# Layer 3: biases folded into the weights' last row, and a second bank for the attention sums

## The chip, the cores and the metric

The kernel runs on one core of one Trainium2 chip. The metric is the device time of one execution in microseconds; the median of three runs stands for a kernel. A core has five engines with instruction queues of their own: PE (matrix multiply, with its weight loads shown apart as PEld), DVE (vector), ACT (scalar functions), POOL (GpSimd) and SP (which issues most DMAs here). PE writes its results to PSUM, which the kernel uses as eight banks of 512 fp32 values per partition.

## The reference, cut to what matters

The model has four layers over x of shape (4, 56, 56, 128): 4 images of 3136 tokens with 128 channels. Layers 0 to 2 (neighbourhood attention; a selective scan; additive attention and a layer of 64 experts that choose their tokens) are not changed. Layer 3 is:

```python
t = t + _L3_attn_ref(_ln_t(t))     # softmax(x x^T) x, per image
t = t + _L3_ffn_ref(_ln_t(t), router_w, router_b, expert_w, expert_b)

def _L3_ffn_ref(x, router_w, router_b, expert_w, expert_b):     # 8 experts, the best 2 of a token
    router_probs = softmax(x @ router_w + router_b, axis=-1)
    top_p, top_i = top_k(router_probs, 2)
    top_p = top_p / sum(top_p, axis=-1, keepdims=True)
    expert_out = einsum('bnd,edc->bnec', x, expert_w) + expert_b
    gathered = take_along_axis(expert_out, top_i[..., None], axis=2)
    return einsum('bnk,bnkc->bnc', top_p, gathered)
```

`_ln_t` subtracts the mean over the channels and divides by the deviation, without a gain or an offset. So the 128 channels of a normalised token add up to zero, and its last channel is minus the sum of the other 127.

## The kernel before

All tokens stay in SBUF as X[b], one tile of [112, 28, 128] fp32 for each image: 28 tiles of 112 tokens. A chunk is four such tiles, 448 tokens; an image has seven (NCH = 7).

The attention of layer 3 (from L1462) works on units (b, c, t): for chunk c of queries and key tile t of 128 keys (25 of them, the last with 64), "weights" (L1545) multiplies the transposed tokens to scores in a "q" bank, and ACT takes their exp into a tile "e"; "weighted" (L1555) multiplies the keys by e into the sums "o" of the chunk, over 25 units into one bank. The pool of "o" has one bank (L1485), that of "q" two, "m" (shared by transposes and small products) two, "pe" (experts) two, and "h" one. The last serves only the pass over layer 2's experts for the last image, which is woven into the first part of layer 3. That makes eight.

The order on PE, ACT, DVE and POOL is written out by hand. A list `at` holds steps by slot; the loop (L1593) runs in each turn u the scores of unit u, the sums of unit u - 2, and then the steps of slot u - 2. A chunk's steps start in the slot of its last unit:

- slot 0, "copied" (L1530): the sums leave their bank, the first half by DVE (L1533), the second by ACT (L1534). Slots 2 and 3, "added" (L1536): transposed back by matmuls with "back" (L1149), divided, added to X.
- slots 4 to 12, "normed_chunk" (L1609): statistics, root, Newton step, norm of the tokens (slot 8), transposes (slot 11), copy by ACT to f_xT.
- slots 14 to 17: the router's matmuls with addition of its bias and the maximum ("route", L1663), exp, and the choice of two experts, which makes the gate, an [112, 4, 8] tile with zeros for the experts not chosen ("choose", L1687).
- slot 22, "turn_gate" (L1703): four transposes of the gate on PE; slot 23: ACT copies them to gT; slot 25, "biases" (L1714): four matmuls of gT with the experts' biases, and one DVE addition to X.
- slots 25, 27, 29 and 31, "experts" (L1722): for each of the four tiles, two matmuls against four experts at a time, and eight gated additions to X on DVE (L1731). Slot 33: the chunk is stored.

A chunk has 25 slots, so slots 25 and up fall together with the next chunk's slots 0 and up, and stand ahead of them in the same slot. Each fp32 matmul appears in the trace as two instructions.

The next image's chunks are prepared (normed_chunk, then "keys", L1510) during the present image. The pass over layer 2's experts is fed in by a counter u, at half a slot or more per step (L1587), and ends in slot 291 of some 730.

The weights of layer 3 are loaded by SP in L1472 to L1480. Before the loop stands a start (L1565 to L1567), in which the first image's seven chunks are normed and turned, one after the other.

Of the kernel before, what the change touches and what calls it, by code (L numbers as in the profile page):

```python
# [11 lines left out]
ALU = mybir.AluOpType  # L12
AX = mybir.AxisListType
PSUM = bass.MemoryType.PSUM
# [3 lines left out]
B, HW, C = 4, 56, 128  # L18
S = HW * HW
P = 128  # L20
TP = 2 * HW
NT = S // TP
TC = 4
CH = TC * TP
# [28 lines left out]
E3, K3 = 8, 2  # L53
# [51 lines left out]
class Hybrid:  # L105
# [1356 lines left out]
    def layer3(self):  # L1462
# [6 lines left out]
        with ExitStack() as ctx:  # L1469
            wp = ctx.enter_context(tc.tile_pool(name="l3_w", bufs=1))  # L1470
            w = {}
            w["rw"] = self.load(wp, [P, E3], "rw", a["L3_ffn_router_w"])  # L1472
            w["rb"] = self.load(wp, [TP, E3], "rb", a["L3_ffn_router_b"].partition_broadcast(TP))
            w["ew"] = self.load(wp, [P, E3, C], "ew", a["L3_ffn_expert_w"].rearrange("e d c -> d e c"))
            w["eb"] = self.load(wp, [E3, C], "eb", a["L3_ffn_expert_b"])
            shift = self.t(wp, [P, 1], "shift")
            nc.vector.memset(shift, SHIFT3)
            w["eps"] = self.t(wp, [TP, 1], "eps3")
# [5 lines left out]
            ps_q = ctx.enter_context(tc.tile_pool(name="l3_q", bufs=2, space=PSUM))  # L1484
            ps_o = ctx.enter_context(tc.tile_pool(name="l3_o", bufs=1, space=PSUM))  # L1485
            ps_m = ctx.enter_context(tc.tile_pool(name="l3_m", bufs=2, space=PSUM))
            ps_h = ctx.enter_context(tc.tile_pool(name="l3_h", bufs=1, space=PSUM))
            ps_e = ctx.enter_context(tc.tile_pool(name="l3_e", bufs=2, space=PSUM))
            ctx.enter_context(
                tc.manual_schedule(engines={ET.PE, ET.Activation, ET.DVE, ET.Pool})  # L1490
            )
# [62 lines left out]

            def weighted(b, c, t):  # L1555
                if t == 0:
                    po[b, c] = self.t(ps_o, [P, 512], "o")[:, :CH]
                n = tiles[t][1]
                nc.tensor.matmul(  # L1559
                    po[b, c], xk[b][:n, t, :], es.pop((b, c, t))[:n], start=(t == 0), stop=(t == N - 1)  # L1560
                )

            table()
            at = {}
# [23 lines left out]
            for steps, num in ((chosen, 4), (passed, 2)):  # L1588
                for n, step in enumerate(steps):
                    at.setdefault(u // den, []).append(step)  # L1590
                    u += 0 if step.holds else num
            assert u // den < 2 * NCH * N + 6
            for u in range(max(at) + 3):  # L1593
                if u < len(units):
                    weights(*units[u])
                if 0 <= u - 2 < len(units):
                    weighted(*units[u - 2])
                for step in at.get(u - 2, []):
                    step()
# [6 lines left out]
        nc.vector.tensor_scalar(q, q, -0.5, 1.5, op0=ALU.mult, op1=ALU.add)  # L1606
        nc.vector.tensor_mul(g, g, q)

    def normed_chunk(self, b, c, sm, m, eps, turned):  # L1609


        nc = self.nc
        x = self.X[b]
        r = {}

        def stats():
            r["mv"] = self.t(sm, [TP, TC, 2], "lc_mv", bufs=4)
            for k in range(TC):
                st = self.t(sm, [TP, nc.vector.BN_STATS_DIM], "ln_st", bufs=4)
                nc.vector.bn_stats(st, x[:, TC * c + k, :])  # L1620
                nc.vector.bn_aggr(r["mv"][:, k, :], st)


        def root():
            r["r"] = g = self.t(sm, [TP, TC], "lc_r", bufs=4)
            nc.scalar.activation(g, r["mv"][:, :, 1], AF.Ln, bias=eps)
            nc.scalar.activation(g, g, AF.Exp, scale=-0.5)

        def newton():
            self.newton(r["r"], self.t(sm, [TP, TC], "lc_q"), r["mv"][:, :, 1])  # L1630

        def norm():
            r["xa"] = self.t(sm, [TP, TC, C], "lc_xa", bufs=4)
            for k in range(TC):
                nc.vector.tensor_scalar(
                    r["xa"][:, k, :], x[:, TC * c + k, :], r["mv"][:, k, 0:1], r["r"][:, k : k + 1],
                    op0=ALU.subtract, op1=ALU.mult,
                )

        def turn():  # L1640
            r["ps"] = ps = m()
            for k in range(TC):
                nc.tensor.transpose(
                    ps[:, k * TP : (k + 1) * TP], r["xa"][:, k, :], self.ident[:TP, :TP]
                )

        return [
            (0, stats), (2, root), (3, newton), (4, norm), (7, turn), (8, lambda: turned(r["ps"]))
        ]

    def token_choice(self, b, c, w, sm, m, ps_e):

        nc = self.nc
        tile4 = lambda tag, n: self.t(sm, [TP, TC, n], tag)
        per_token = lambda ap: ap.unsqueeze(2).to_broadcast([TP, TC, E3])
        x4 = self.X[b][:, TC * c : TC * (c + 1), :]
        r = {}

        def turned(ps):
            r["xT"] = self.t(sm, [P, CH], "f_xT")  # L1660
            nc.scalar.copy(r["xT"], ps[:, :CH])

        def route():  # L1663
            ps = m()
            for k in range(TC):
                nc.tensor.matmul(
                    ps[:TP, k * E3 : (k + 1) * E3], r["xT"][:, k * TP : (k + 1) * TP], w["rw"],
                    start=True, stop=True,
                )


            r["pr"] = pr = tile4("r_pr", 2 * E3 - K3)
            nc.gpsimd.memset(pr[:, :, E3:], NOTHING)
            r["p8"] = p8 = pr[:, :, 0:E3]
            nc.vector.tensor_tensor(
                p8, ps[:TP, : TC * E3].rearrange("p (t e) -> p t e", e=E3),
                w["rb"].unsqueeze(1).to_broadcast([TP, TC, E3]), op=ALU.add,
            )
            r["red"] = red = self.t(sm, [TP, TC], "r_red")
            nc.vector.tensor_reduce(red, p8, axis=AX.X, op=ALU.max)  # L1680
            nc.vector.tensor_tensor(p8, p8, per_token(red), op=ALU.subtract)

        def exp():
            nc.scalar.activation(r["p8"], r["p8"], AF.Exp)


        def choose():  # L1687
            top, rest = tile4("r_top", 8), tile4("r_rest", 2 * E3 - K3)
            r["gate"] = gate = tile4("r_gate", E3)
            for k in range(TC):  # L1690
                nc.vector.max(top[:, k, :], r["p8"][:, k, :])
            nc.vector.tensor_add(r["red"], top[:, :, 0], top[:, :, 1])
            nc.vector.reciprocal(r["red"], r["red"])
            nc.vector.memset(top[:, :, K3:], NOTHING)
            for k in range(TC):
                nc.vector.match_replace(
                    out=rest[:, k, :], in_to_replace=top[:, k, :], in_values=r["pr"][:, k, :],
                    imm_value=0.0,
                )
            nc.vector.tensor_sub(gate, r["p8"], rest[:, :, 0:E3])  # L1700
            nc.vector.tensor_tensor(gate, gate, per_token(r["red"]), op=ALU.mult)

        def turn_gate():  # L1703
            r["pg"] = pg = m()
            for k in range(TC):
                nc.tensor.transpose(
                    pg[:E3, k * TP : (k + 1) * TP], r["gate"][:, k, :], self.ident[:TP, :TP]
                )

        def turned_gate():  # L1710
            r["gT"] = self.t(sm, [E3, CH], "gT")
            nc.scalar.copy(r["gT"], r["pg"][:E3, :CH])

        def biases():  # L1714
            pb = m().rearrange("p (k c) -> p k c", c=C)
            for k in range(TC):
                nc.tensor.matmul(
                    pb[:TP, k, :], r["gT"][:, k * TP : (k + 1) * TP], w["eb"], start=True, stop=True
                )
            nc.vector.tensor_add(x4, pb[:TP], x4)  # L1720

        def experts(k):  # L1722
            x = x4[:, k, :]
            for e0 in range(0, E3, 4):
                pe = self.t(ps_e, [P, 4, C], "pe")
                nc.tensor.matmul(  # L1726
                    pe[:TP].rearrange("p e c -> p (e c)"), r["xT"][:, k * TP : (k + 1) * TP],
                    w["ew"][:, e0 : e0 + 4, :].rearrange("p e c -> p (e c)"), start=True, stop=True,
                )
                for e in range(4):  # L1730
                    nc.vector.scalar_tensor_tensor(  # L1731
                        x, pe[:TP, e, :], r["gate"][:, k, e0 + e : e0 + e + 1], x,
                        op0=ALU.mult, op1=ALU.add,
                    )

        def store():
            dst = self.out[b].rearrange("h w c -> (h w) c").rearrange("(t p) c -> p t c", p=TP)
            nc.sync.dma_start(out=dst[:, TC * c : TC * (c + 1), :], in_=x4)

        bind = lambda f, *args: lambda: f(*args)  # L1740
        return (
            self.normed_chunk(b, c, sm, m, w["eps"], turned)
            + [(10, route), (12, exp), (13, choose), (18, turn_gate), (19, turned_gate), (21, biases)]
            + [(21 + 2 * k, bind(experts, k)) for k in range(TC)] + [(21 + 2 * TC, store)]
        )

# [42 lines left out]
```

## Time and profile before

| what | value |
|---|---|
| median of 3 runs | 8328.65 us (8322.74 to 8329.06) |
| the profiled execution | 8338.93 us, of which the span from first to last instruction is 8337.2 |
| layer 3's first load | at 6728.66 us of the span |
| first "q" matmul of layer 3 | at 6761.07 |
| pass over layer 2's experts: last addition to X | at 7440.66 |
| last "o" group begins | at 8287.39 |
| last store is issued | at 8333.86 |
| granted PE clock over the span | 0.924 of full |

Busy time by engine over the whole span: PE 7035.0 us, DVE 6274.1, ACT 5125.5, POOL 2902.1. These are averages over four layers with different limits, so the prediction cuts layer 3 out first. In the timelines each line is one group of equal instructions: when it started, how long it took in all, engine, line of the kernel, operation, out<-in, and in brackets the idle time ahead of it with the engine that ended it. [...]

### The profile page before, as it was taken

The page shows a single profiled execution, that of the slowest core. Times are in us where ns is not written, and L with a number is a line of the kernel's source. Part 1 is how long each engine was busy: PE and PEld are TensorE (multiplying, and loading weights), DVE is VectorE, ACT ScalarE, POOL GpSimd, SP SyncE. Part 2 cuts the span into 40 slices and gives each one's busy share as a digit, 9 for nine tenths or more (in the row PEclk, how much of TensorE's full clock was granted, in tenths as well). Part 3 has the DMA queues.
Part 4 walks back from the last instruction along what each step waited for, and adds up shares of the span by engine and source line. Part 5 has one row for each costly group of instructions (what it writes and reads, how often), then busy time and mean ns, then how long its engine had stood idle before and what let it go on. Part 6 is the DMA issues. An engine that isn't in the chain of part 4 may idle for free.

```text
span 8337.2 us, 109252 instructions
## 1 busy us (share of the span) xinstructions
PE 7035.0 (84%) x41373; PEld 2773.9 (33%) x41373; DVE 6274.1 (75%) x12303; ACT 5125.5 (61%) x5001; POOL 2902.1 (35%) x1997
## 2 busy tenths in 40 slices
PE   8878998999899999996777777777777889999998
PEld 4432333333333332332222222222222344454444
DVE  6768998999898899897777878777787754344434
ACT  4445555555455555554998799889889964333332
POOL 4537876877677768772000000000001000000000
PEclk9988998999898889897999999999999989999999
DMA  2000000000000000000000000000003101210000
GB/s 51 1 13 1 1 1 1 1 1 1 1 1 1 1 1 1 1 1 5 1 1 1 5 1 1 1 5 1 1 25 113 44 4 54 86 44 5 5 5 6
DMA packets 84469, 102.05 MB, mean 12 GB/s; under 512 B 21132, under 2 KB 49700, under 8 KB 83236
## 3 DMA queue, kind: packets, MB, share of 16 engines
q1 hardware_dynamic: 83941, 95.06, 3.8%
q8 instruction: 327, 5.36, 0.3%
q14 instruction: 201, 1.64, 0.1%
HBM read 84.76 MB, written 10.29 MB: 11 GB/s over the span
## 4 chain that ended last, share of the span: by engine, by line
PE 48%; ACT 21%; DVE 20%; issue 9%; POOL 1%; SPq 0%; ACTq 0%; DMA 0%; DVEq 0%; POOLq 0%
ACT th L1021 12%; DVE hs L672 7%; PE q L1548 6%; PE o L1559 6%; PE a L650 6%; PE s L1032 5%; PE m L779 5%; DVE th L1012 5%; PE y L682 3%; PE o L1059 2%; PE pe L1726 2%; PE u L657 2%; DVE e L428 2%; DVE dBu L667 2%; PE m L808 1%
## 5 line engine op out<-in xcount | busy, mean ns | idle before, releaser
L1021 ACT ACTIVATE th<-th 128x3136 f32<-128x3136 f32 (+12 forms) x1120 | 2293.3, 2094 | 217.6 <-DVE th L1012 169.2
L1012 DVE TENSOR_SCALAR th<-fT,g 128x784 f32<-128x784 f32 (+6 forms) x3920 | 1934.3, 561 | 468.2 <-PE s L1032 440.5
L676 POOL TENSOR_TENSOR hs<-hs,bc 128x896 f32<-128x896 f32 x896 | 1859.0, 2084 | 688.8 <-DVE hs L672 578.3
L1032 PE MATMUL s<-th,place 128*32 128x392 f32 (+7 forms) x14336 | 1487.7, 491 | 714.5 <-ACT th L1021 711.1
L672 DVE TENSOR_TENSOR_SCAN hs<-a,dBu 128x448 f32<-128x448 f32 x1792 | 1845.1, 1070 | 160.8 <-POOL hs L676 87.4
L660 ACT ACTIVATE a<-a 128x896 f32<-128x896 f32 x896 | 808.5, 902 | 931.2 <-PE u L657 431.0
L650 PE MATMUL a<-delta,A_pick 32*128 32x448 f32 x3584 | 1080.3, 638 | 97.0 <-DVE hs L672 93.1
L657 PE MATMUL u<-du,pick 32*128 32x448 f32 x3584 | 1033.8, 656 | 26.7 <-DVE dBu L667 22.6
L667 DVE TENSOR_TENSOR dBu<-u,bc 128x448 f32<-128x448 f32 x1792 | 1014.1, 606 | 45.8 <-PE u L657 40.8
L1032 PEld LDWEIGHTS s<-th,place 128*32 128x32 f32 (+1 forms) x14336 | 423.0, 111 | 1648.8 <-ACT th L1021 1130.5
L1553 ACT ACTIVATE e<-q,shift 128x448 f32<-128x448 f32 (+1 forms) x700 | 443.0, 634 | 774.3 <-PE q L1548 774.0
L1559 PE MATMUL o<-e,xk 128*128 128x448 f32 (+1 forms) x1400 | 657.3, 551 | 61.4 <-ACT oT L1534 61.4
L1548 PE MATMUL q<-xT 128*128 128x448 f32 (+1 forms) x1400 | 656.1, 551 | 7.7 <-ACT e L1553 7.7
L1050 POOL TENSOR_TENSOR e<-e,later 112x112 f32<-112x112 f32 x112 | 79.6, 710 | 1589.8 <-ACT e L1043 961.9
L650 PEld LDWEIGHTS a<-delta,A_pick 32*128 32x128 f32 x3584 | 338.3, 202 | 706.8 <-issue 327.5
L682 PE MATMUL y<-hs,sum 128*32 128x448 f32 x3584 | 494.4, 626 | 3.6 <-POOL hs L676 3.6
L1731 DVE SCALAR_TENSOR_TENSOR X<-pe,r_gate,X 112x128 f32<-112x128 f32 x896 | 313.8, 350 | 188.9 <-PE pe L1726 153.4
L1059 PE MATMUL o<-e,xa 112*128 112x392 f32 (+5 forms) x1024 | 418.5, 531 | 1.1 <-POOL e L1050 1.1
L657 PEld LDWEIGHTS u<-du,pick 32*128 32x128 f32 x3584 | 299.5, 204 | 297.4 <-DVE dBu L667 294.5
L1559 PEld LDWEIGHTS o<-e,xk 128*128 128x128 f32 (+1 forms) x1400 | 262.0, 192 | 351.8 <-issue 273.5
L1548 PEld LDWEIGHTS q<-xT 128*128 128x128 f32 (+1 forms) x1400 | 248.8, 189 | 235.4 <-issue 218.7
L1522 POOL MEMSET xk<- 128x4 f32 (+1 forms) x28 | 2.9, 105 | 847.0 <-DVE xk L1521 701.2
(263 smaller groups left out, 7959.4 us busy)
## 6 DMA issues: line engine op xcount, KB each, us to landing
wide<-in_L_ffn_weight SPq DMA_DIRECT2D x64, 1024.0 KB
X<-in_x SPq DMA_DIRECT2D x8, 784.0 KB
out<-X SPq DMA_DIRECT2D x28, 224.0 KB
M<-wide SPq DMA_DIRECT2D x4, 784.0 KB
wide<-M SPq DMA_DIRECT2D x4, 784.0 KB
e_edge<-dtab SPq DMA_DIRECT2D x42, 49.0 KB
cw<-in_L_conv_conv_w SPq DMA_DIRECT2D x1, 1024.0 KB
c_h<-in_L_ffn_weight SPq DMA_DIRECT2D x16, 64.0 KB
```

Source lines behind the costliest of these rows:

```text
L650: nc.tensor.matmul(A[p][:, k], w["A"][own, l, f, q, :], pre[j]["delta"][own, f], start=True, stop=True,)
L657: nc.tensor.matmul(U[p][:, k], w["pick"][own, q, :], pre[j]["du"][own, f], start=True, stop=True)
L660: nc.scalar.activation(A[p], A[p], AF.Exp)
L667: nc.vector.tensor_mul(V[p][:, k], u[:, k], pre[p // PAIRS]["bc"][:, 0])
L672: nc.vector.tensor_tensor_scan(HS[p][:, k], A[p][:, k], V[p][:, k], 0.0, op0=ALU.mult, op1=ALU.add)
L676: nc.gpsimd.tensor_mul(HS[p], HS[p], bc[:, 1:2].to_broadcast([P, 2, CH]))
L682: nc.tensor.matmul(py[j, f][r * HD : (r + 1) * HD, :], w["sum"][:, q, :], HS[p + r // 2][:, r % 2], start=False, stop=(q == QG - 1),)
L1012: nc.vector.tensor_scalar(th[i][:, blk, lo:hi], fT[j][:, lo:hi], im[order[j][0]]["g"][:, at : at + 1], None, op0=ALU.add,)
L1021: nc.scalar.activation(own, own, AF.Tanh)
L1032: nc.tensor.matmul(ps[j, J][QW * blk : QW * blk + rows, h, lo:hi], place[:, off : off + rows], z[:, blk, h * HALF + lo : h * HALF + hi], s ...
L1548: nc.tensor.matmul(ps[:n, :CH], xT[b][:, k : k + n], xT[b][:, c * CH : (c + 1) * CH], start=True, stop=True,)
L1559: nc.tensor.matmul(po[b, c], xk[b][:n, t, :], es.pop((b, c, t))[:n], start=(t == 0), stop=(t == N - 1))
```

## The change

The router's and the experts' biases move into the weights. From every row of the expert weights (per channel d) the row of channel 127 is subtracted, and likewise for the router; then row 127 itself is overwritten by the bias. The tokens that go to router and experts get 1.0 in channel 127. Since the channels of a normalised token add up to zero, the product is the same as before with the bias added. The tiles rb and eb, the steps turn_gate, turned_gate and biases, and the router's addition go.

Beside this, the PSUM pool "h" is closed one slot behind the last step of the pass over layer 2's experts, and a pool "l3_o2" is opened in its place. From then on a chunk's sums take one of two banks by the parity of c.

```diff
             w["rw"] = self.load(wp, [P, E3], "rw", a["L3_ffn_router_w"])
-            w["rb"] = self.load(wp, [TP, E3], "rb", a["L3_ffn_router_b"].partition_broadcast(TP))
             w["ew"] = self.load(wp, [P, E3, C], "ew", a["L3_ffn_expert_w"].rearrange("e d c -> d e c"))
-            w["eb"] = self.load(wp, [E3, C], "eb", a["L3_ffn_expert_b"])
+            with ExitStack() as tmp:
+                tp = tmp.enter_context(tc.tile_pool(name="l3_tmp", bufs=1))
+                last = self.load(
+                    tp, [P, E3, C], "ew_last", a["L3_ffn_expert_w"][:, C - 1, :].partition_broadcast(P)
+                )
+                nc.vector.tensor_sub(w["ew"], w["ew"], last)
+                rlast = self.load(
+                    tp, [P, E3], "rw_last", a["L3_ffn_router_w"][C - 1, :].partition_broadcast(P)
+                )
+                nc.vector.tensor_sub(w["rw"], w["rw"], rlast)
+            nc.sync.dma_start(out=w["ew"][C - 1 : C, :, :], in_=a["L3_ffn_expert_b"].unsqueeze(0))
+            nc.sync.dma_start(out=w["rw"][C - 1 : C, :], in_=a["L3_ffn_router_b"].unsqueeze(0))
...
-            ps_h = ctx.enter_context(tc.tile_pool(name="l3_h", bufs=1, space=PSUM))
             ps_e = ctx.enter_context(tc.tile_pool(name="l3_e", bufs=2, space=PSUM))
+            spare = ctx.enter_context(ExitStack())
+            ps_h = spare.enter_context(tc.tile_pool(name="l3_h", bufs=1, space=PSUM))
+            sums = [ps_o]
...
             def weighted(b, c, t):
                 if t == 0:
-                    po[b, c] = self.t(ps_o, [P, 512], "o")[:, :CH]
+                    po[b, c] = self.t(sums[c % len(sums)], [P, 512], "o")[:, :CH]
...
+            def passed_by():
+                spare.close()
+                sums.append(spare.enter_context(tc.tile_pool(name="l3_o2", bufs=1, space=PSUM)))
+
+            at.setdefault(u // den + 1, []).append(passed_by)
...
         def norm():
...
+            if ones:
+                nc.gpsimd.memset(r["xa"][:, :, C - 1 : C], 1.0)
...
         def route():
...
-            nc.vector.tensor_tensor(
-                p8, ps[:TP, : TC * E3].rearrange("p (t e) -> p t e", e=E3),
-                w["rb"].unsqueeze(1).to_broadcast([TP, TC, E3]), op=ALU.add,
-            )
+            logits = ps[:TP, : TC * E3].rearrange("p (t e) -> p t e", e=E3)
             r["red"] = red = self.t(sm, [TP, TC], "r_red")
-            nc.vector.tensor_reduce(red, p8, axis=AX.X, op=ALU.max)
-            nc.vector.tensor_tensor(p8, p8, per_token(red), op=ALU.subtract)
+            nc.vector.tensor_reduce(red, logits, axis=AX.X, op=ALU.max)
+            nc.vector.tensor_tensor(p8, logits, per_token(red), op=ALU.subtract)
...
-        def turn_gate():
...
-        def turned_gate():
...
-        def biases():
...
-            + [(10, route), (12, exp), (13, choose), (18, turn_gate), (19, turned_gate), (21, biases)]
+            self.normed_chunk(b, c, sm, m, w["eps"], turned, ones=True)
+            + [(10, route), (12, exp), (13, choose)]
```

Only the tokens for router and experts ask for `ones`; the preparation for the attention does not.

More of the change, by code (lines that the diff above doesn't have):

```diff
@@ L1607, in newton, with normed_chunk @@
         nc.vector.tensor_mul(g, g, q)
-    def normed_chunk(self, b, c, sm, m, eps, turned):
+    def normed_chunk(self, b, c, sm, m, eps, turned, ones=False):
         nc = self.nc
@@ L1701, in choose @@
             nc.vector.tensor_tensor(gate, gate, per_token(r["red"]), op=ALU.mult)
-        def turn_gate():
[L1704 to L1708, printed above, removed]
-        def turned_gate():
-            r["gT"] = self.t(sm, [E3, CH], "gT")
-            nc.scalar.copy(r["gT"], r["pg"][:E3, :CH])
-        def biases():
[L1715 to L1720, printed above, removed]
         def experts(k):
@@ L1741, in token_choice @@
         return (
-            self.normed_chunk(b, c, sm, m, w["eps"], turned)
-            + [(10, route), (12, exp), (13, choose), (18, turn_gate), (19, turned_gate), (21, biases)]
+            self.normed_chunk(b, c, sm, m, w["eps"], turned, ones=True)
+            + [(10, route), (12, exp), (13, choose)]
             + [(21 + 2 * k, bind(experts, k)) for k in range(TC)] + [(21 + 2 * TC, store)]
```

## The prediction

> **What bounds the kernel now.** The change touches only layer 3, so I first cut the trace by stretch of time: the busy time of each engine from layer 3's first load to its first score matmul, from there to the end of the pass over layer 2's experts (its last addition to X starts at 7440.66), on to the last "o" matmul, and the tail.
>
> ```profile
> core 0: us, PE busy (x) PEld busy (x) DVE busy (x) ACT busy (x) POOL busy (x), PEclk, DMA share, GB/s
> 6728.00:6761.00 33.00, 13.67 (x55) 10.04 (x56) 26.03 (x123) 24.65 (x35) 0.52 (x5) 0.50 0.07 19
> 6761.00:7445.00 684.00, 651.78 (x2605) 327.58 (x2604) 298.43 (x1167) 264.71 (x455) 32.27 (x139) 0.98 0.18 56
> 7445.00:8290.00 845.00, 807.57 (x2463) 406.22 (x2461) 343.53 (x1403) 292.73 (x529) 2.50 (x25) 0.99 0.02 5
> 8290.00:8337.20 47.20, 27.55 (x73) 11.40 (x72) 30.71 (x111) 2.13 (x6) 0.00 (x0) 0.74 0.04 10
> ```
>
> From 6761 to 8290 PE is busy 95% of the time, DVE and ACT 42% and 36%: PE sets the pace, so every instruction taken from it shortens the span. In the 33 us start and the 47 us tail it does not. Second, PE's waits from 6761 to 8290:
>
> ```profile
> engine line waited for: us in total, times, longest us
> PE o L1559 <- ACT oT L1534: 61.4, 26, 3.0
> PE q L1548 <- ACT e L1553: 7.7, 8, 3.9
> PE m L1643 <- DVE lc_xa L1635: 0.6, 1, 0.6
> ```
>
> One wait recurs: the first "o" of a chunk waits until the sums of the chunk before are out of their one bank. Third, one such place in order of time:
>
> ```profile
> 8240.25 1.12 PE L1717 MATMUL m<-eb,gT 8*112 8x128 f32 x8
> 8241.30 1.97 PE L1726 MATMUL pe<-ew,f_xT 128*112 128x512 f32 x4
> 8242.45 3.12 DVE L1731 SCALAR_TENSOR_TENSOR X<-pe,r_gate,X 112x128 f32<-112x128 f32 x8 [0.35 <-PE pe L1726]
> 8243.11 0.92 PE L1548 MATMUL q<-xT 128*128 128x448 f32 x2
> 8245.49 0.38 DVE L1533 COPY oT<-o 128x224 f32<-128x224 f32 x1
> 8245.96 0.35 ACT L1534 COPY oT<-o 128x224 f32<-128x224 f32 x1 [5.91 <-DVE oT L1533]
> 8246.35 1.02 PE L1559 MATMUL o<-e,xk 128*128 128x448 f32 x2 [2.33 <-ACT oT L1534]
> 8247.21 0.92 PE L1548 MATMUL q<-xT 128*128 128x448 f32 x2
> ```
>
> In the chunk's last slot stand the biases and first experts of the chunk before, ahead of "copied". DVE reaches the copy only after eight gated additions, ACT copies after DVE, PE stands idle.
>
> [...]
>
> **The change part by part.** All sums are against the profiled execution, 8338.93 us (span 8337.2); the median of the runs is 8328.65, 10.28 lower, and I carry the same difference over.
>
> (a) Gate transposes and bias matmuls leave PE. A row's busy time overlaps, so I price them by start to start. Biases: 8240.25 to 8241.30, 1.05 us a chunk. Gate transposes: at 8286.01, the next "q" at 8286.49, 0.48 us; the "q" to "o" step behind them is 0.90 where it is otherwise 0.84 for that 64-column tile (6851.17 to 6852.01): 0.54 in all. Twenty-six bias groups and 27 gate groups lie ahead of 8290, the rest in the tail: 26 x 1.05 + 27 x 0.54 = 27.3 + 14.6 = 41.9 us. The ends: 35 if some of it falls where PE would wait for another engine anyway in the pass, 46 if changes of weight shape come off as well. The DVE addition (0.69 us), router addition (0.19) and ACT copy of gT (0.505) that go with them lie beside PE's work and are worth nothing there.
>
> (b) The second bank. `passed_by` stands one slot after the pass: with 60 choice slots (14 holding, 4 units each) and 200 expert slots (9 holding, 2 units), u reaches 582, slot 291, so it runs in loop turn 294. Chunks are 25 turns long; the first whose sums start later is number 12 of 0 to 27 (image 1, c = 5). From there the bank is c % 2, and c = 6 to c = 0 of the next image both take bank 0: of 16 transitions two keep the wait, 14 lose it. The cost of one is the "q" to "q" time around it, 8243.11 to 8247.21, 4.10, less the plain 1.50: 2.60 us. What is late next? ACT's copy holds up the later exps. Counted from the first expert matmul, it ends at 8246.31 - 8241.30 = 5.01 us. PE meanwhile has experts, q, o, q, o (1.81 + 4 x 0.75 = 4.81) and the next four expert matmuls (about 1.8) ahead of the first instruction that needs oT, at 6.6, and of the first "q" that needs a held-up exp, at 7.0; that exp is done by about 5.6. So 1.3 us of margin, and 14 x 2.60 = 36.4 us. The ends: 0 if another wait takes its place each time, 38 with the longer stalls.
>
> (c) The ones in xa. A POOL memset (0.10 us, by the row of xk L1522) now stands between norm and the token transposes. After the pass norm ends at 8265.04 and the transposes start at 8268.28: 3.2 us of cover, against 0.10 and two handovers. POOL is free there (2.5 of 845 us). In the pass it also fills z; the margin is similar (7187.8 to 7190.78), except in the first chunk, at 6886.00, where PE starts right behind the first of four norms: 0.8 us lost once. Without that cover each of 27 chunks would lose about 0.9, 24 us: my bound. Behind the waiting transposes everything on PE would queue.
>
> (d) The start. DVE gains two subtractions, ew (128x1024) and rw (128x8). Price of the first: [...] the trace's additions (192 ns for 32 elements, 691 for 512) extrapolate to 1.22. With rw 1.4 us. The data: ew is issued at 6729.54 and its bytes are through by about 6733.3:
>
> ```profile
> 6731.00:6732.00 1.00, 0.00 (x0) 0.00 (x0) 0.93 (x6) 0.77 (x1) 0.00 (x0) 0.50 0.64 165
> 6732.00:6733.00 1.00, 0.00 (x0) 0.00 (x0) 0.60 (x4) 0.97 (x3) 0.00 (x0) 0.50 1.12 338
> 6733.00:6734.00 1.00, 0.00 (x0) 0.00 (x0) 0.00 (x0) 1.00 (x1) 0.00 (x0) 0.50 0.24 66
> ```
>
> [...] The last rows cost as many bytes again, so about 6737 for the pair. If DVE takes the subtractions when they are ready, it loses 1.4 us in a stretch where DVE and ACT are both nearly full. If they stand ahead of the first statistics (6729.40), it waits from there: about 9. The memsets of L1477 and L1479 ran before a reciprocal that the program has ahead of them, so work outside the fixed order is put where it is ready: I take 2.0, range 0 to 9. The xT tile may reuse their scratch space; its first write is at 6740.51, late enough. SP holds the two row-127 loads and then "back" behind the subtraction; "back" is first needed near 6805.
>
> (e) The tail. The bias group at 8290.04 leaves: 1.05. Router addition: 0.22. The gate is ready at 8315.81, the additions start at 8321.54, since transposes, copy, biases and their addition come between; the expert matmuls then stand ready on PE, so 5.7, and the 0.2 gap before 8323.24. Against that the memset delays the transposes, which now overlap norm (8308.84 to 8309.96): 0.8. Sum 6.4, range 4 to 8.
>
> Total: 41.9 + 36.4 - 0.8 - 2.0 + 6.4 = 81.9 us. Profiled 8338.93 - 81.9 = 8257.0; median 8328.65 - 81.9 = 8246.8.
>
> **The rivals.** R1: the bank brings nothing, because the wait moves to a "q" held up by ACT or a transpose that wants oT. For it: ACT's copy still comes after eight DVE additions. Against: the 1.3 us margin. Total 45.5: 8283. R2: half of (a) is lost, PE idling elsewhere in the pass, where other engines also serve the choice of tokens. Against: only 8.3 us of other PE waits. Total 61: 8268. R3, slower: the granted PE clock, 0.98 and 0.99 in the two long stretches, drops as the idle gaps go. The 1447 us that would be left there lengthen in proportion: at 0.91 instead of 0.985 by 1447 x (0.985 / 0.91 - 1) = 119, giving 8366; it decides from about 0.93, where the 82 are gone. For it: earlier slices of the page show 0.8 and 0.9. Against: those slices are not fuller, and 8000 to 8200 shows 1.00 with PE busy 95%. That the bank does not do what it says in 13 of 27 transitions is already in the sum.
>
> **How the numbers follow.** Forecast 0.76, R1 0.10, R2 0.09, R3 0.03, and 0.02 for no change by a mishap of the start or placement that I do not see. The likeliest case's own range: (a) 35 to 46, (c) to (e) -7 to +4 around the sum, some 3 us between medians: 8235 to 8262. Taking in R2 and a weaker form of R1 it is 8232 to 8272. About 0.2%, 17 us, is what a measurement tells from no change: faster 0.95 (forecast, R1, R2), same 0.03 (the mishaps and a third of R3), slower 0.02.
>
> **What would show it.** The stretch after the pass should shrink from 845 to about 783 (14 x 2.60 and 16 bias and gate groups, 62 us), the wait of "o" for oT from 26 times to about 12 and 61 to about 29 us, with no new PE wait over 5 us in total; the tail from the last "o" to the end from 47 to about 41; first "q" at 6763 instead of 6761. Wrong would be: waits of "m L1149" or "q" of 2 us a chunk (R1), transposes waiting for POOL, a clock under 0.97 (R3), or a start later by 5 us and more.

## The result and the profile after

The changed kernel takes 8254.67 us (median of 4 runs, 8244.34 to 8260.68), the kernel before on the same chip 8325.69 (4 runs, 8322.29 to 8329.06): ratio 0.9913, 95% interval 0.9896 to 0.9931, 71 us less. The forecast was 82 us less.

The two profiled executions differ by more, 8337.2 against 8242.6 us of span. 20 us of that lie in layers 0 to 2, which the change doesn't touch: layer 3's first memset comes at 6728.7 before and 6708.6 after. So the change must be read from layer 3 alone: 1608.5 us before, 1534.0 after, 74.5 less. First the view by stretch of the kernel after, cut at the same events as before (first "q", the end of the pass over layer 2's experts, the last chunk's end):

```profile
core 0: us, PE busy (x) PEld busy (x) DVE busy (x) ACT busy (x) POOL busy (x), PEclk, DMA share, GB/s
6708.00:6744.00 36.00, 14.33 (x56) 10.05 (x56) 27.41 (x125) 24.64 (x35) 0.55 (x6) 0.50 0.14 32
6744.00:7422.00 678.00, 643.79 (x2484) 316.94 (x2483) 289.46 (x1145) 260.22 (x444) 32.85 (x148) 0.97 0.17 56
7422.00:8200.60 778.60, 773.93 (x2268) 384.75 (x2266) 329.70 (x1371) 283.79 (x512) 4.33 (x42) 1.00 0.02 5
8200.60:8242.60 42.00, 25.03 (x53) 8.95 (x52) 29.26 (x108) 1.61 (x5) 0.21 (x2) 0.74 0.04 12
```

The stretch behind the pass fell from 845 to 779 us, where 783 was forecast, and PE is busy 99% of it. The pass fell only from 684 to 678. PE's granted clock moved as well: 0.98 to 0.97 in the pass, 0.99 to 1.00 behind it. PE's waits in these two stretches:

```profile
engine line waited for: us in total, times, longest us
PE o L1574 <- ACT oT L1549: 29.3, 12, 3.6
PE q L1563 <- ACT e L1568: 7.6, 8, 3.4
PE m L1667 <- POOL r_pr L1697: 1.5, 1, 1.5
```

The wait of "o" for the copy went from 26 times to 12, and no new wait of more than 1.5 us in all came in its place. One chunk's end in the last image, in order of time:

```profile
8107.64 1.97 PE L1728 MATMUL pe<-ew,f_xT 128*112 128x512 f32 x4
8108.79 3.12 DVE L1733 SCALAR_TENSOR_TENSOR X<-pe,r_gate,X 112x128 f32<-112x128 f32 x8 [13.04 <-PE pe L1728]
8109.45 0.91 PE L1563 MATMUL q<-xT 128*128 128x448 f32 x2
8110.20 0.92 PE L1574 MATMUL o<-e,xk 128*128 128x448 f32 x2
8110.95 0.92 PE L1563 MATMUL q<-xT 128*128 128x448 f32 x2
8111.83 0.38 DVE L1548 COPY oT<-o 128x224 f32<-128x224 f32 x1
8112.30 0.34 ACT L1549 COPY oT<-o 128x224 f32<-128x224 f32 x1 [4.87 <-DVE oT L1548]
8114.17 0.60 PE L1149 MATMUL m<-back,oT 128*112 128x129 f32 x4
```

DVE still copies behind its eight additions, but "o" no longer waits: it begins 0.75 us after "q". The first instruction that needs oT, at 8114.17, comes 1.5 us after ACT's copy ends.

For the experiments I cut every trace in the same way, from the start times of its instructions (chunks are counted from 0 to 27; the "pass" here ends with chunk 12's first "o", a little later than in the view above): "start" is from layer 3's first memset to the first "q", "pass" from there to the first "o" of chunk 12, "behind" from there to the last "o", "tail" the rest. The clock records of the traces of before and after have PE at 1.0 or at 0.5 of full clock and nothing between; the last two columns are the time at half clock in "pass" and "behind". All in us:

| kernel | layers 0-2 | start | pass | behind | tail | half, pass | half, behind |
|---|---|---|---|---|---|---|---|
| before | 6728.7 | 32.3 | 700.6 | 827.9 | 47.6 | 26.0 | 17.1 |
| after | 6708.6 | 35.2 | 691.1 | 765.2 | 42.4 | 40.3 | 3.4 |
| e1, no bank | 6716.7 | 35.1 | 693.6 | 810.8 | 42.3 | 40.3 | 27.3 |
| e2, bank only | 6728.8 | 32.3 | 698.1 | 787.2 | 48.2 | 26.1 | 3.4 |
| e3, copy in front | 6717.0 | 34.9 | 650.2 | 758.3 | 42.3 | 9.8 | 0.0 |
| e4, the same, no bank | 6718.7 | 34.6 | 648.0 | 758.3 | 42.0 | 6.8 | 0.0 |
| e8, before, copy in front | 6727.1 | 32.3 | 663.0 | 780.3 | 47.3 | 9.0 | 0.0 |
| e6, subtractions on POOL | 6731.8 | 33.6 | 685.8 | 765.2 | 42.4 | 28.2 | 3.4 |
| e9, four edits | 6724.3 | 33.6 | 648.7 | 758.3 | 42.0 | 7.7 | 0.0 |
| e10, e4 with gate transposes | 6723.3 | 34.9 | 653.5 | 764.5 | 44.0 | 9.8 | 0.0 |
| e11, after with gate transposes | 6735.7 | 34.5 | 688.2 | 771.4 | 44.9 | 27.3 | 3.4 |

What was open: why the pass won 9.5 us where the forecast gave 19.3 (11 gate and bias groups of 1.59, which is how many lie in it, and chunk 12's wait of 2.60, less 0.8), and whether the second bank, or something simpler, is what the wait asks for.

### The profile page after: what moved, and what is told of

It is laid out like the page before. It is cut to its first block, busy times and chain, and to the rows that moved or that the text cites. A ratio compares the mean times of both kernels' runs of the same rounds, so it can differ in the third digit from the quotient of the medians.

```text
span 8242.6 us, 108525 instructions
## 1 busy us (share of the span) xinstructions
PE 6973.4 (85%) x41037; PEld 2728.2 (33%) x41037; DVE 6250.8 (76%) x12249; ACT 5109.7 (62%) x4973; POOL 2901.2 (35%) x2025
## 4 chain that ended last, share of the span: by engine, by line
PE 46%; ACT 21%; DVE 17%; issue 9%; POOL 1%; DMA 0%; SPq 0%; ACTq 0%; DVEq 0%; POOLq 0%
ACT th L1021 13%; PE q L1563 6%; DVE hs L672 6%; PE o L1574 6%; PE a L650 6%; PE s L1032 5%; PE m L779 5%; DVE th L1012 4%; PE y L682 3%; PE o L1059 2%; PE pe L1728 2%; PE u L657 2%; DVE dBu L667 2%; PE m L808 1%; PE y L690 1%
## 5 line engine op out<-in xcount | busy, mean ns | idle before, releaser
L1032 PE MATMUL s<-th,place 128*32 128x392 f32 (+8 forms) x14336 | 1487.7, 491 | 714.4 <-ACT th L1021 711.1
```

Source lines behind the costliest of these rows:

```text
L1032: nc.tensor.matmul(ps[j, J][QW * blk : QW * blk + rows, h, lo:hi], place[:, off : off + rows], z[:, blk, h * HALF + lo : h * HALF + hi], s ...
```

## The experiments

### Is the second bank worth what it was priced at?

e1 is the changed kernel without the line that opens the bank:

```diff
-            at.setdefault(u // den + 1, []).append(passed_by)
```

> The changed kernel with the second bank never opened: all 28 chunks keep their one bank for the sums, everything else of the change stays. My theory (the bank takes away 14 waits of 2.60 us, and nothing takes their place): 36 us slower than the changed kernel, so about 8291, up to 8298 if PE also spends more time at half clock because of the waits. Rival (the bank only moved the wait): less than 12 us slower, 8255 to 8267. In the trace the wait of 'o' for oT is back in 26 places.

Measured: 8303.66 us (9 runs), ratio to before 0.9972, interval 0.9961 to 0.9982. That is 49 us above the changed kernel's median, more than the 36 to 43 expected. In the table "behind" grew by 45.6, "pass" by 2.5. Chunk by chunk (first "o" to first "o") most chunks behind the pass take 48.05 us with the bank (47.26 in the last image), and without it 2.60 more, the price of the wait, or some 4.3 more: 50.65 or 52.34. Half clock in "behind" went from 3.4 to 27.3 us. So the bank takes away two things, the waits and the stretches of half clock that come with them.

e2 is the kernel before with the bank alone (pool "h" closed behind the pass, "l3_o2" opened, sums by the parity of c).

> The kernel before with the second bank alone; biases and gate transposes stay. My theory: 36 us less than before, 8289, with a second 'o' bank from chunk 12 on and 12 waits left. If the two halves of the change help each other (the bias matmuls stand in front of the copy, so they could cover part of the wait), the gain is smaller than 30.

Measured: 8289.45 us (4 runs), ratio 0.9955, interval 0.9940 to 0.9970, 39.6 us less than before, as expected. Chunks 15 and 16 (from their first "o" to the next chunk's) took 52.08 and 53.67 us in the kernel before, here 49.48 and 49.37. The first pair of numbers differs by 2.60, the second by 4.30.

### Why the pass won so little

e3 is the changed kernel with one edit: the step that empties the sums' bank goes to the front of its slot, ahead of the experts of the chunk before.

```diff
-                        at.setdefault(u + N - 1 + k, []).append(step)
+                        to = at.setdefault(u + N - 1 + k, [])
+                        to.insert(len(to) if k else 0, step)
```

> The changed kernel, with the step that empties the sums' bank put in front of the biases' and experts' steps of its slot. Theory: the wait exists only because the copy stands behind eight gated additions on DVE; in front of them it ends about 1 us after the last 'o', under 2.5 us of PE work, so the waits left in the pass (11 of 2.60 us) and at two image borders go, and with them windows of half PE clock: 29 + 5 + 5 to 12 us less than the changed kernel, 8209 to 8216. Rival for the pass, where the change won half of what I forecast (other engines set the pace there): the pass shrinks by less than 15 us, 8235 or more. In the trace the time at half clock in the pass should fall from 51 us to under 35.

Measured: 8205.94 us (4 runs), ratio 0.9857, interval 0.9843 to 0.9872, 3 us below the theory's 8209 to 8216 and far from the rival's 8235. (The 51 us at half clock named there are 40.3 when cut as in the table; they fell to 9.8.) The pass went from 691.1 to 650.2: 40.9 us. Ten waits at 2.60 explain 26.0 of it (the expectation counted eleven, but the first chunk has none), and the 30.5 us less at half clock, counted as half lost, another 15.3; the sum is 41.3. (That half is the author's estimate, from the chunks of e1: 1.70 us more with 3.413 us at half clock.) So the bulk of what the pass kept was these waits and the half clock, and not other engines.

How waits and clock hang together shows in the kernel after around the wait that ends at 7257.77, in four neighbouring stretches of about 3.4 us:

```profile
7251.80:7255.20 3.40, 3.40 (x9) 1.26 (x8) 1.24 (x4) 0.63 (x1) 0.00 (x0) 1.00 0.00 0
7255.20:7258.55 3.35, 1.01 (x3) 0.30 (x2) 1.87 (x6) 0.88 (x2) 0.00 (x0) 1.00 0.01 2
7258.55:7261.95 3.40, 3.40 (x11) 1.04 (x11) 0.00 (x0) 0.00 (x0) 0.00 (x0) 0.50 0.03 8
7261.95:7265.35 3.40, 3.40 (x12) 1.71 (x11) 1.27 (x4) 0.63 (x1) 0.00 (x0) 1.00 0.85 305
```

(Columns as in the view by stretch; the clock is the third number from the end.) The second stretch holds the wait, PE is busy 1.01 us of it. The third runs at half clock though PE is busy throughout, the fourth at full clock again. In layer 3 of the traces of before and after the clock's changes lie 3.413 us apart or a multiple of it, to 0.001 us; such a stretch is called a window here. In the pass of the kernel after, nine of the ten waits have a half-clock stretch that begins between 0.4 us ahead of their end and 1.3 us after it; in the kernel before it is five of the same ten. The length of a wait did not decide whether one followed: chunks 15 to 19 of the kernel before begin with waits of equal length (2.33 to 2.34 us) and alternate between 52.08 us without and 53.67 us with. In the kernel after, the wait that ends at 7533.53 (2.34 us) is followed by no half clock; two windows share it:

```profile
7528.20:7531.61 3.41, 3.00 (x7) 1.00 (x6) 1.75 (x5) 0.07 (x1) 0.00 (x0) 1.00 0.00 0
7531.61:7535.02 3.41, 1.49 (x4) 0.87 (x5) 1.35 (x4) 0.88 (x2) 0.00 (x0) 1.00 0.00 0
7535.02:7538.43 3.41, 3.41 (x13) 1.71 (x12) 1.37 (x4) 0.63 (x1) 0.00 (x0) 1.00 0.00 0
```

All eleven traces, cut into these windows from the first "q" to the last "o", agree: of 4585 windows at full clock, every one in which PE was busy 1.37 us or less was followed by a window at half clock, and none with 1.49 us or more was; three lay between (1.41 to 1.44), and one of them was. In all 68 were followed by one. In the traces of before and after alone it was 22 of 848: PE was busy 0.30 to 1.44 us in the 22, and at least 1.49 us in the others. These are counts; what sets the clock, no run here tests. Half of 3.413 us is 1.71, and the chunks with and without a window at half clock differ by 1.70 (52.34 and 50.65 in e1, last digits rounded).

e11 moves the waits against this window: the changed kernel with the gate transposes and their copy put back in each chunk, with nothing that reads them.

> The changed kernel with the same transposes put back, to move the spacing of the waits in the pass a little. In the changed kernel chunks 8 to 11 take 57.9 us on average, nearly 17 of the clock's 3.413 us windows (58.02), and every wait there falls so that a window at half clock follows. Theory: it depends on how the waits lie to those windows. If the spacing stays locked, the pass gets 4 to 6 us longer and keeps about 51 us at half clock; if it gets out of step, half-clock time falls under 45 and the pass gets longer by less than 3 us. Rival (half clock in the pass has nothing to do with the waits' spacing): 51 us at half clock, and the pass longer by 12 times the gate's price.

Measured, in a single run: 8276.56 us. The pass is 2.9 us shorter than in the changed kernel, 688.2, though PE has 11 x 0.38 = 4.2 us more work in it (e10 below has the 0.38); half clock went from 40.3 to 27.3, by the same estimate worth 6.5 us. That fits the theory: 4.2 - 6.5 = -2.3. The pass is not longer by the gate's price, so the rival falls. (Here too the 51 in the expectation means 40.3.)

The length of a chunk alone does not decide it, though. e6, further down, has the chunks of the changed kernel as they are and only a start that is 1.6 us shorter; half clock in its pass is 28.2 us, and six of the same ten waits have such a stretch behind them, where the changed kernel has nine. Where start and pass are the same, the table's figure comes again: 26.0 and 26.1 (before and e2), 40.3 and 40.3 (after and e1).

### What the biases and transposes were worth, apart from the clock

e8 is the kernel before with the copy in front and nothing else. Against e4 (below) it isolates the work taken from PE, for neither has the waits.

> The kernel before, with nothing but the sums' copy put in front of the biases and experts of its slot. It has no waits of 'o', and so hardly any windows of half PE clock, as the same edit gave in the changed kernel; against that run it shows what leaving the biases and gate transposes off PE is worth when the clock doesn't disturb. Theory (the forecast of 1.05 + 0.54 us a chunk was right, and the clock took 7 us of it back in the pass): stretch from first 'q' to last 'o' longer by 42 less 2 us of new POOL waits, about 17 us of that in the pass; total about 43 us above the changed kernel with the copy in front and no second bank, 8246. Rival (half of it is lost in the pass, where other engines set the pace): difference in the pass 9 us or less, total 8236 or less.

Measured: 8252.85 us (4 runs), ratio 0.9900, interval 0.9883 to 0.9916, against 0.9851 (0.9837 to 0.9866) of e4. The difference in the ratios, 0.0049, is about 41 us; 43 were expected. From first "q" to last "o" the traces differ by 1443.3 - 1406.3 = 37.0 us; 40 were expected. The pass has 15.0 of them: more than the rival's 9, less than 17. Behind the pass every chunk differs by 1.43 or 1.44 (49.48 against 48.05, 48.69 against 47.26), not by the 1.59 of the forecast.

e10 splits that: e4 with the gate transposes and their ACT copy put back.

> Copy in front, no second bank, and the gate's transposes with their ACT copy put back in each chunk; nothing reads what they make. It splits the 1.43 us a chunk that leaving both groups out was measured to be worth: with the forecast price of 0.54 us for the transposes a chunk takes 48.05 + 0.54 = 48.59 us (and the biases are then worth 0.89 instead of 1.05); if the bias price of 1.05 is right, it takes 48.43. Stretch from first 'q' to last 'o': 15 us more than without them in the first case, 10 in the second.

Measured: a chunk takes 48.43 us, 0.38 more. So the transposes are worth 0.38, not 0.54, and the biases, by difference, 1.43 - 0.38 = 1.05, as forecast. "Pass" and "behind" together are 11.7 us longer (1418.0 against 1406.3; the half-clock time is 3 us higher too).

### Is the bank needed at all?

e4 is e3 without the second bank: the copy in front, and one bank for the sums to the end.

> As the run before, without the second bank. Theory: with the copy in front the one bank is free in time, so the second bank is worth nothing: within 0.2% of the run before, 8209 to 8220. Rival: one bank still makes 'o' wait, by 1 us or more a chunk, 25 us and more above the run before.

Measured: 8203.03 us (4 runs), ratio 0.9851, interval 0.9837 to 0.9866; e3 had 8205.94 on the same chip. "Behind" is 758.3 us in both. In order of time:

```profile
8067.09 1.97 PE L1728 MATMUL pe<-ew,f_xT 128*112 128x512 f32 x4
8067.20 0.39 DVE L1548 COPY oT<-o 128x224 f32<-128x224 f32 x1 [12.00 <-PE o L1574]
8067.62 0.35 ACT L1549 COPY oT<-o 128x224 f32<-128x224 f32 x1 [0.74 <-DVE oT L1548]
8068.90 0.92 PE L1563 MATMUL q<-xT 128*128 128x448 f32 x2
8069.65 0.92 PE L1574 MATMUL o<-e,xk 128*128 128x448 f32 x2
```

The copies end at 8067.97, while PE still has experts and a "q" ahead of the "o" at 8069.65: 1.7 us to spare. With the order mended, the bank of the change is worth nothing that these runs can tell. This version is also faster than both kernels, by 1.5% against before and by about 0.6% against after.

### The start and the tail

The start of the kernel after, DVE and SP in order of time:

```profile
6709.45 0.57 SPq L132 DMA_DIRECT2D ew_last<-in_L_ffn_expert_w  x1
6718.35 1.23 DVE L1481 TENSOR_TENSOR ew<-ew,ew_last 128x1024 f32<-128x1024 f32 x1 [2.41 <-DMA ew_last<-in_L_ffn_expert_w]
6719.50 0.16 DVE L1485 TENSOR_TENSOR rw<-rw,rw_last 128x8 f32<-128x8 f32 x1
6719.57 0.34 DVE L1656 TENSOR_SCALAR lc_xa<-X,lc_mv,lc_r 112x128 f32<-112x128 f32 x1
6719.97 0.18 PEld L1667 LDWEIGHTS m<-ident,lc_xa 112*128 112x128 f32 x1 [3.79 <-DVE lc_xa L1656]
```

The subtractions stand between the third and the fourth norm of the first chunk. DVE gets there early and waits 2.41 us for the rows, until 8.9 us after their issue.

e6 gives the two subtractions to POOL, which has nothing to do there.

```diff
-                nc.vector.tensor_sub(w["ew"], w["ew"], last)
+                nc.gpsimd.tensor_sub(w["ew"], w["ew"], last)
...
-                nc.vector.tensor_sub(w["rw"], w["rw"], rlast)
+                nc.gpsimd.tensor_sub(w["rw"], w["rw"], rlast)
```

> The changed kernel with the two subtractions of the weights on POOL instead of DVE. Theory (DVE waits 2.4 us for the last rows at the start, with the norm of the second tile group queued behind): the start, from layer 3's first memset to the first 'q', goes from 35.2 us back to 32.3 to 33.2. Rival (the transfers themselves disturb the start): it stays at 35.

Measured, in a single run: the start is 33.6 us. That is less of a gain than was expected, but 1.6 below 35.2, so the rival falls. The total, 8260.52, is no measure of it (its layers 0 to 2 took 23 us more than in the profile of the kernel after, and its pass had 12 us less at half clock). Why not all of it came back, the timeline of e6 shows:

```profile
6741.38 2.34 POOL L1481 TENSOR_TENSOR ew<-ew,ew_last 128x1024 f32<-128x1024 f32 x1 [19.05 <-DMA back<-in_k_out]
6741.44 2.29 DVE L1628 TENSOR_TENSOR lc_r<-lc_r,lc_q 112x4 f32<-112x4 f32 x1
6743.67 0.20 POOL L1485 TENSOR_TENSOR rw<-rw,rw_last 128x8 f32<-128x8 f32 x1
6743.77 1.12 DVE L1656 TENSOR_SCALAR lc_xa<-X,lc_mv,lc_r 112x128 f32<-112x128 f32 x4
```

A DVE product of four elements per partition, 0.16 us elsewhere, took 2.29 us (6741.44 to 6743.73), beside POOL's subtraction of 2.34 us (6741.38 to 6743.72). In e9, which follows, it took 2.34 us beside 2.34.

e9 puts together the copy in front, one bank, the subtractions on POOL, and the ones written by DVE:

```diff
-                nc.gpsimd.memset(r["xa"][:, :, C - 1 : C], 1.0)
+                nc.vector.memset(r["xa"][:, :, C - 1 : C], 1.0)
```

> Copy in front, no second bank, subtractions on POOL, and the ones written by DVE right behind the norm instead of by POOL. Theory: 2.4 us of start, 1.5 us of one POOL wait in the pass and 0.3 us of the tail better than without the last two edits, about 8199; by the median of a few runs that can't be told from 8203, so the stages of the trace decide.

Measured: ratio 0.9846, interval 0.9831 to 0.9860 (8210.02 us on a chip where the kernel before takes 8339.49); e4 has 0.9851. By stages: start 33.6 against 34.6, pass 648.7 against 648.0, tail 42.0 in both. The last two edits together win nothing to speak of, against 4.2 us expected. With the ones on DVE, PE's wait for them in the pass is 1.45 us where it was 1.54, and the tail is the same: the transposes wait for the last of four norms and its ones, wherever these are written.

## Why the prediction was right, and where its terms were off

The prediction held as a whole: the forecast was 8246.8, measured 8254.67, inside the range, by the mechanism named. In layer 3 alone the forecast of 81.9 us stands against 74.5. The sum is closer than its terms, in part by luck: two effects of the clock that it didn't price, of about 7 us each, cancel. Its terms:

- **(a) Gate and bias groups, 41.9 forecast.** The bias group's 1.05 was right (e8 and e10). The mis-sized term is the gate's 0.54 us a chunk, read as 0.48 from start to start plus 0.06 for a slower step behind it; e10 measured 0.38. The same place in e4, without the transposes:

```profile
8062.05 0.97 PE L1563 MATMUL q<-xT 128*64 128x448 f32 x2
8062.94 1.02 PE L1574 MATMUL o<-e,xk 128*128 128x448 f32 x2
```

The step from this 64-column "q" to "o" is 0.90 us without them too, so the 0.06 was not theirs; the 0.84 that it was compared with stands where the "q" follows another 64-column matmul. And 0.09 of the 0.48 is the step from "o" into the 64-column tile: without transposes it takes 0.47 us from the last "o" instruction, 0.38 between equal tiles. That is 27 x 0.16 = 4.3 us too much. Another 1.8 us were not won in the pass, where chunks 1, 2, 3, 5 and 11, with the clock's part taken out, gain less than the 1.43 of the others. 0.6 of that is chunk 3's wait for its copy, 3.6 us where it was 3.0; what took the rest stays open.

- **(b) The bank, 36.4 forecast.** The wait's price of 2.60 us is exact (52.08 against 49.48), and 14 waits went. What the prediction didn't price is the half-clock stretch behind some of these waits: 17.1 us of it became 3.4 behind the pass, by the estimate of a half worth another 6.9. The margin of 1.3 us for what is late next held; R1 was wrong.
- **The pass.** It won 9.5 instead of 19.3. The forecast allowed for PE idling on other engines there (R2); that is at most the 1.8 us in (a). The larger cause is the clock: half clock in the pass rose from 26.0 to 40.3 us, by the same estimate a loss of 7.2 us, for nine of the ten waits there had a half-clock stretch with them, where five of the ten had before. Shorter chunks and a longer start (35.2 against 32.3 us) both moved these waits; in e6, with a start of 33.6 us and the changed kernel's chunks, it was six of ten and 28.2 us, so the start alone moved them too. The two were not separated. It is chance that the loss about cancels the gain behind the pass.
- **R3** had the direction of the clock wrong behind the pass: as the gaps went, it rose from 0.99 to 1.00. In the pass it fell from 0.98 to 0.97, but by where the gaps lie that stayed, not because gaps went.
- **(c) The ones, 0.8 once.** Not paid. PE's wait in front of the transposes at that place is 1.54 us where it was 0.55, but from the start of the first norm there to the "q" that PE next waits for it is 5.39 us (6869.23 to 6874.62), as it was 5.40 before (6885.63 to 6891.03): that "q" waits for an exp of ACT either way. No other chunk shows such a wait, as the 3 us of cover said.
- **(d) The start, 2.0 with a range of 0 to 9.** 2.9 (35.2 against 32.3). The subtractions cost 1.23 and 0.16 us, as priced; the rows could be used at 6718.3, some 9.7 us behind the memset, where the forecast had 8.3, and DVE stood waiting instead of taking them when ready. The forecast let the second load take about as long as the first (some 3.8 us, 6729.54 to 6733.3, the author's estimate); it was waited for until 8.9 us after its issue (6709.45 to 6718.35).
- **(e) The tail, 6.4 forecast.** 5.2 (47.6 to 42.4). The bias group (1.05), the gate path and the 0.8 us for the later transposes came as forecast: the additions start 6.1 us earlier after the last "o". Missed is that then PE's refills come late twice, 0.59 and 0.20 us, where the forecast had no such gap left; and the stretch behind the last addition is 0.2 us longer: 1.0 of the 1.2.

Together: 4.3 and 1.8 in (a), 0.9 in (d), 1.2 in (e) and about 0.3 net of the clock, less 0.8 in (c), makes 7.7, against the 7.4 us between forecast and trace. The rest between 74.5 and the medians' 71 lies within the scatter of layers 0 to 2, of which the profiles of eleven kernels show 6708.6 to 6735.7 us. They too go with the clock: 1146 us of half clock in the profile at 6708.6, 1205 in that at 6735.7, 58 us more half clock for 27.1 us more time.

Not tried: a smaller transfer of the last rows (one row loaded and spread on the chip), and opening the bank by the parity over all chunks alone; e3 made the second pointless.

## What to carry to other kernels

Where an engine waits for a buffer, look first at what stands ahead of the freeing instruction on its engine: here moving two copies ahead of eight additions took another 0.6% off the changed kernel (0.9857 against 0.9913), and made the second bank useless. A wait on PE cost more than its length here where a half-clock stretch followed: 2.60 us for the wait and another 1.70 for the stretch (e1). Count both, and read the effect of an edit in the stretch that it touches, not in totals whose untouched part scatters by 27 us. To price a removed instruction group, put it back alone in an otherwise undisturbed stretch: a reading of start times counted the step into a 64-column tile as the group's, and was off by 0.16 of 0.54 us.

## What the runs showed of the hardware that was not expected

- The half clock went with PE's busy time in windows of 3.413 us, not with waits as such. In the eleven traces every window at full clock in which PE was busy 1.37 us or less was followed by one at half clock, even where PE was busy all through that one (3.40 of 3.40 us from 7258.55 in the kernel after); with 1.49 us or more none was (68 followed of 4585; before and after alone 22 of 848). The chunks with such a window took 1.70 us more (e1). A wait of 2.34 us that left PE busy 1.01 us in its window was followed by one (it ends at 7257.77 in the kernel after), a wait of 2.34 us that left PE busy 3.00 and 1.49 us in two windows was not (it ends at 7533.53). In the pass it was five of ten waits in the kernel before, nine in that of the kernel after, and six in e6, with the same chunks and a start 1.6 us shorter.
- A DVE product of four elements per partition, 0.16 us elsewhere, took 2.29 us while POOL subtracted for 2.34 (e6), and 2.34 beside 2.34 (e9). Why, no run here tests.
